# Down in two float32r passes for eight of eleven pieces, weights remade in tiles 2 to 7, x's row addition on GpSimd and one reciprocal for h and x

## The chip, the cores and the metric

The kernel runs on one core of one Trainium2 chip. The metric is the device time of the whole program in microseconds (us); the time before is 1699.41 us, the median of three runs (1698.96 to 1700.25). Engines are named as in the profile: PE is TensorE (PEld its weight loads), DVE is VectorE, ACT is ScalarE, POOL is GpSimd, and SP issues most DMAs. L1069 is line 1069 of the kernel file.

## What is computed

One block of a network: a gated linear scan, and then a feed-forward part whose rows and weights are rounded to FP4 in blocks of 16 values. Both are added to x through modulation vectors. Cut to what the change touches:

```
def fp4_quant_dequant(x):          # blocks of 16 along the last dim
    scale = max(abs(x) over the block) / 6, at least 1e-12
    xn = x / scale
    return GRID[searchsorted(MID, abs(xn))] * sign(xn) * scale

def fp4_linear(x, w):
    return einsum('bsk,nk->bsn', fp4_quant_dequant(x), fp4_quant_dequant(w))

x = x + ga * scan_part(layernorm(x) * (1 + ca) + sa)     # stage 1
h = layernorm(x) * (1 + cb) + sb                         # stage 2
h = silu(fp4_linear(h, w_gate)) * fp4_linear(h, w_up)    # 512 -> 1408
x = x + gb * fp4_linear(h, w_down)                       # 1408 -> 512
```

x has 2 x 4096 rows of 512 float32 values.

## The kernel before

Stage 1 (the scan) takes the first 528 us, and the first rows of x for stage 2 are rounded beside it. The change is in stage 2, the feed-forward part: a loop over 64 tiles of 128 rows. There the order of instructions on every engine, and on the DMA queues of SP and POOL, is the order in which the code issues them (`tc.manual_schedule`); no planner moves anything.

**Values in two parts.** FP4 values times their scales don't fit into one f16 number, so each of h, x and the weights is kept as a high and a low part, both f16. A product of one 128-wide piece of the contraction is then three f16 passes (high x high, high x low, low x high: `PASSES`). Where one side can be held in the type float32r, two passes do it (`TWO`): high x whole and low x remade, with the weights remade so that the cross terms come out right (a factor LAM or LAMX enters both sides).

**PE.** In iteration i PE runs `products(i)` (L1069): gate and up, three column groups of 480, 464 and 464 each, into six PSUM banks, over four pieces of 128. At first all four pieces take three f16 passes (72 matmuls). From tile 5 the last one, two and then three pieces take two float32r passes (`twos`, `wide`, `xw`), so a settled tile has 54. Then `down(i - 2)` (L1190) runs Down of the tile two before: 11 pieces of h, the first eight in three f16 passes and the last three in two f16 passes with LAM: 30 matmuls of 128x512. `hT` holds all of h transposed, both parts.

**The rest of a tile, in order.** ACT applies silu to each group (L1086); DVE makes the three gated products `hid` (L1091), which frees the PSUM banks for the next tile. On POOL, `out_times` (L1246) scales the Down result of an earlier tile, and `x_times` (L1115) multiplies the normalised x of the tile three ahead by its modulation; DVE adds the shift (`x_plus`, L1119). ACT casts the next tile's x to float32r (`xw`, L1050), and takes the mean and spread of the x four tiles ahead (L644, L650); POOL makes rstd and off (L652, L653, L1103).

Then h is rounded: DVE's block maxima (L136), scales `sb` (L117) and reciprocal (L132); ACT sums the scales (L123); POOL inverts the sum (`rt`, L125), makes `sl` in parts of 24 and of 64 columns (L1134, L1135), issues the output's accumulating DMA (`send`, L1232) and subtracts `sh` (L1141). DVE multiplies by the reciprocal (`xn`, L1146), ACT takes the absolute value (L1147), DVE rounds in two steps (L107, L109), ACT spreads the scales over 1024 columns (`se`, L1153, twice), and DVE forms the f16 parts (L1164, L1170, L1176) with one ACT copy between (L1166). SP issues the transpose of the parts (`hT`, L1185).

Between these lie the same steps for the x of the tile two ahead (reciprocal, L681, two roundings, L689, L697, its transpose `x2T` at L699), the block maxima of the x three ahead, and near the end of POOL's row that x's scales: `sb` (L117), then ACT's sum (L123) and `u` (L127), then `rt` and `sl` (L676). ACT reads the Down result from PSUM (`o`, L1241) and normalises the next x (`x_hat`, L1109).

**Remaking weights.** At i = 0, SP copies the gate and up weights to tiles of their own (`move_weights`, L1018), which frees the room for their float32r forms. In tiles 2 to 8 one gate or up piece at a time is remade: DVE adds its parts (L1034), ACT writes the rounded float32r form and a scaled one (L1038, L1039), DVE makes the second form (L1043).

Of the kernel before, what the change touches and what calls it, by code (L numbers as in the profile page):

```python
# [19 lines left out]
P = 128  # L20
D = 512
# [23 lines left out]
LAM = 81.0  # L45
LAMX = 101.0
TWOS = 3
MOVED = 2


@with_exitstack
def tile_adaln_block(
# [62 lines left out]
    def bounded(engine, am, nb):  # L115
        sb = small.tile([P, nb], F32, name="sb", tag=f"sb{nb}", bufs=2)
        engine.tensor_scalar(sb, am, 6e-12, TIE / 6.0, ALU.max, ALU.mult)  # L117
        return sb
# [11 lines left out]
    def inverse(sb, nb):  # L130
        inv = small.tile([P, nb], F32, name="inv", tag=f"inv{nb}", bufs=2)
        V.reciprocal(inv, sb)  # L132
        return inv
# [272 lines left out]
    DOWN = [(k, *p) for k in range(IC) for p in (PASSES if k * P < HSPLIT else TWO)]  # L406
# [122 lines left out]
    def quant_weight(wt, am, col, parts, hl):  # L529
# [17 lines left out]
        for at, by in parts:  # L547
            if by is None:
                A.copy(b1[:, at], xn[:, at])
            else:  # L550
                A.activation(b1[:, at], xn[:, at], AF.Copy, scale=by)
# [3 lines left out]
    def quant_rows(wt, i, am, col):  # L555
        dst = weights(("wgT", "wuT")[col], col, [P, 2 * KC, INTER])
        hl = new_hl()
        yield from quant_weight(wt, am, col, [(slice(0, D), None)], hl)
        S.dma_start_transpose(dst[:, :, i * P : (i + 1) * P], flat(hl))
# [6 lines left out]
    def quant_down(wt, i, j):  # L566
        n0, n1 = CHUNKS[j]
        w = n1 - n0
        dst = weights("wdT", 2, [P, 2 * IC, D])
        hl = flat(new_hl())[:, : 2 * w]  # L570
        two = hl.rearrange("p (a d) -> p a d", a=2)
        by = None if n0 < HSPLIT else (LAM - 1.0) / LAM
        yield from quant_weight(wt, am_d[i][j], 2, [(slice(0, w), by)], two)
        c = wd_chunk(0, n0 // P)
        S.dma_start_transpose(dst[:, c : c + 2 * w // P, i * P : (i + 1) * P], hl)
# [50 lines left out]
    NS = NBLK * KC  # L626
    qx, x1s, xst, gbs = {}, {}, {}, {}
# [31 lines left out]
    def twos(i):  # L659
        return min(max((i - MOVED - 1) // 2, 0), TWOS)  # L660

# [10 lines left out]
    def x_scales(h, am):  # L672
        sb = bounded(G, am, NBX)
# [3 lines left out]
        return h, sb, st, u  # L677

    def x_unit(h, sb, st, u):
        xn = work.tile([P, D], F32, name="xn", tag="xn512", bufs=1)  # L680
        V.tensor_tensor(blocks(xn), blocks(h), spread(inverse(sb, NBX), NBX), ALU.mult)  # L681
# [19 lines left out]

    ahead = {}

    def x_early(i, stage):
        if stage == 0:
            ahead[i] = x_scales(*x_norm(i))
        elif stage == 1:
            ahead[i] = x_unit(*ahead[i])
# [5 lines left out]
    EARLY = {NS - 3: [(0, 1)], NS - 2: [(0, 3), (1, 1)], NS - 1: [(1, 3)]}  # L714
    LATE = {NS - 4: [(0, 0)], NS - 3: [(0, 2), (1, 0)], NS - 2: [(1, 2)], NS: [(2, 0)]}
# [185 lines left out]
    with order:  # L901
# [3 lines left out]
        for slot in range(KC, NS + 3):  # L905
# [83 lines left out]
            if NS - 5 <= slot < NS - 1:  # L989
                n = slot - NS + 5  # L990
                xst[n] = stats_x(x1s[n])
            for n, stage in LATE.get(slot, []):
                x_early(n, stage)
            gate = cur
    tc.no_sync_barrier()
# [35 lines left out]
    def widen_sum(k, m):  # L1031
        hi, lo = moved[k][m]
        cv = ring.tile([P, INTER], F32, name="cv", tag="xnh")
        V.tensor_tensor(cv, hi, lo, ALU.add)  # L1034
        return k, m, cv

    def widen_high(k, m, cv):
        A.copy(wide[k][m][0], cv)  # L1038
        A.activation(cv, cv, AF.Copy, scale=LAMX)  # L1039

    def widen_low(k, m, cv):
        b1, b2 = wide[k][m]
        V.scalar_tensor_tensor(out=b2, in0=b1, scalar=1.0 - LAMX, in1=cv, op0=ALU.mult, op1=ALU.add)  # L1043

    def widen_rows(i):
        n = twos(i)
        if n:
            x2T = qx[i][0]
            xw = gring.tile([P, 2, n, P], F32R, name="xw", tag="xw", bufs=2)
# [30 lines left out]
    def brief():  # L1080
        return gring.tile([P, D], F32, name="silu", tag="silu", bufs=3)
# [18 lines left out]
    def x_off(i):  # L1100
        nm, rstd = xst[i]
        off = small.tile([P, 1], F32, name="off", tag="off")
        G.tensor_tensor(off, nm, rstd, ALU.mult)  # L1103
        xst[i] = rstd, off

    def x_hat(i):
        rstd, off = xst.pop(i)
        h = x1s.pop(i)
        A.activation(h, h, AF.Identity, bias=off, scale=rstd)  # L1109
        return i, h  # L1110

    def x_times(i, h):
        scale, by = mods_for(i * P // N)
        xm = brief()
        G.tensor_tensor(xm, h, scale, ALU.mult)  # L1115
        return h, xm, by

    def x_plus(h, xm, by):
        V.tensor_tensor(h, xm, by, ALU.add)  # L1119
# [4 lines left out]
    hb = HSPLIT // QB  # L1124

    def h_max(hid):
        am = small.tile([P, NBH], F32, name="amh", tag="amh", bufs=1)
        block_max(am, hid)
        return hid, bounded(V, am, NBH)

    def h_scales(sb):
        rt, u = total(sb, NBH, ud, 1)
        sl = small.tile([P, NBH], F32, name="sl", tag=f"sl{NBH}", bufs=2)
        G.tensor_scalar(sl[:, hb:], sb[:, hb:], rt, WPEAK * LAM, ALU.mult, ALU.mult)  # L1134
        G.tensor_scalar(sl[:, :hb], sb[:, :hb], rt, None, ALU.mult)  # L1135
        return rt, sl, u

    def h_parts(sb, rt, sl):
        sh = small.tile([P, hb], BF16, name="sh", tag="shh", bufs=2)
        A.activation(sh, sb[:, :hb], AF.Copy, scale=rt)  # L1140
        G.tensor_tensor(sl[:, :hb], sl[:, :hb], sh, ALU.subtract)  # L1141
        return sh

    def h_unit(hid, sb):
        xn = ring.tile([P, INTER], F32, name="xn", tag="xnh")
        V.tensor_tensor(blocks(xn), blocks(hid), spread(inverse(sb, NBH), NBH), ALU.mult)  # L1146
# [3 lines left out]
    def h_spread(sh, sl):  # L1150
        se = ring.tile([P, 2, HSPLIT], F16, name="se", tag="se")
        for n, src in enumerate((sh, sl[:, :hb])):
            A.activation(blocks(se[:, n, :]), spread(src, hb), AF.Copy, scale=WPEAK)  # L1153
            yield se
# [7 lines left out]
    def h_value(xn, nq, sl):  # L1162
        v = xn[:, HSPLIT:]
        V.tensor_tensor(blocks(v), blocks(nq[:, HSPLIT:]), spread(sl[:, hb:], NBH - hb), ALU.mult)  # L1164
        hl = ring.tile([P, 2, INTER], F16, name="hhl", tag="hhl")
        A.activation(hl[:, 0, HSPLIT:], v, AF.Copy, scale=1.0 / LAM)  # L1166
        return v, hl

    def h_low(i, nq, v, hl, se, u):
        V.tensor_tensor(  # L1170
            hl[:, :, :HSPLIT],
            nq[:, :HSPLIT].unsqueeze(1).to_broadcast([P, 2, HSPLIT]),
            se,
            ALU.mult,
        )
        V.scalar_tensor_tensor(  # L1176
            out=hl[:, 1, HSPLIT:],
            in0=hl[:, 0, HSPLIT:],
            scalar=1.0 - LAM,
            in1=v,  # L1180
            op0=ALU.mult,
            op1=ALU.add,
        )
        hT = ring.tile([P, 2 * IC, P], F16, name="hT", tag="hT", bufs=2)
        S.dma_start_transpose(hT, flat(hl))  # L1185
        qh[i] = hT, u

    def down_part(hT, pd, d):
        for n, (k, hp, wp) in enumerate(DOWN):
            T.matmul(  # L1190
                pd,
                hT[:, hp * IC + k, :],
                wdT[:, wd_chunk(wp, k), d],
                start=n == 0,
                stop=n == len(DOWN) - 1,
            )

    def down(i):
        hT, u = qh.pop(i)
        pd = side((P, D))  # L1200
        down_part(hT, pd, slice(0, D))
        return i, pd, u

    def last_down(i):

        hT, u = qh.pop(i)
        b, t0 = divmod(i * P, N)
        o = new_out()
        for n in range(2):
            d = slice(n * D // 2, (n + 1) * D // 2)  # L1210
            pd = bank(n)[:, : D // 2]
            down_part(hT, pd, d)
            scaled(o[:, d], pd, u, gbs[b][:, d])
# [3 lines left out]
    def new_out():  # L1217
        return ring.tile([P, D], F32, name="o", tag="o", bufs=2)

    def scaled(o, pd, u, by):  # L1220
        V.scalar_tensor_tensor(out=o, in0=pd, scalar=u, in1=by, op0=ALU.mult, op1=ALU.mult)  # L1221

    def gain_of(b):
        if b not in gbs:
            t = ring.tile([P, D], F32, name="mod_gb1", tag="mod_gb1")
            S.dma_start(t, modd[5][b : b + 1, :].to_broadcast([P, D]))
            gbs[b] = t
        return gbs[b]
# [4 lines left out]

    def finish(i, pd, u):
        o = new_out()
        scaled(o, pd, u, gain_of(i * P // N))
        send(i, o)
# [6 lines left out]
    def out_times(i, o):  # L1244
        ob = brief()
        G.tensor_tensor(ob, o, gain_of(i * P // N), ALU.mult)  # L1246
        return i, ob

    LAG, LEAD = 2, 2
# [5 lines left out]
    with tc.manual_schedule(engines={V.engine, A.engine, G.engine, S.engine, T.engine}):  # L1255
        ended, widening = [], None
        x = ahead.pop(LEAD)
        x1s[LEAD + 2] = load_x1(LEAD + 2)
        x_off(LEAD + 1)
        hat = x_hat(LEAD + 1)  # L1260
        scaled_out = []
        for i in range(NT):
            last = i == NT - 1
            work_i = products(i)
            downs = [] if i == NT - 2 else [i - LAG - 1, i - LAG] if last else [i - LAG]
# [5 lines left out]
            if i == NT // 4:  # L1271
                mods_for(1)
                gain_of(1)
# [5 lines left out]
            if widening is not None:  # L1279
                widen_high(*widening)  # L1280
            if not last:
# [4 lines left out]
            hid, sb = h_max(work_i[2])  # L1286
# [4 lines left out]
            if widening is not None:  # L1291
                widen_low(*widening)
                widening = None
            for o in outs:
                send(*o)
            xn = h_unit(hid, sb)
            if x is not None:
                x = x_unit(*x)
            sh = h_parts(sb, rt, hs)
            spreading = h_spread(sh, hs)  # L1300
            se = next(spreading)
            if nx is not None:
                nx = x_plus(*nx)
            if x is not None:
                x = x_round(i + LEAD, *x)
            next(spreading)
# [7 lines left out]
            scaled_out = [] if last else [out_of(*e) for e in ended]  # L1314
            hat = x_hat(i + LEAD + 2) if ahead_x else None
            v, hl = h_value(xn, nq, hs)
            h_low(i, nq, v, hl, se, u)
            x = nx
            if 0 <= i - MOVED < 2 * TWOS:
                k, m = KC - 1 - (i - MOVED) // 2, (i - MOVED) % 2  # L1320
                if m == 0:
                    widen_room(k)
                widening = widen_sum(k, m)
        last_x1 = load_x1(NT - 1)
        finish(*ended.pop(0))
        ended.append(down(NT - 2))
# [52 lines left out]
```

## Time and profile before

| | |
|---|---|
| time, median of three runs | 1699.41 us |
| the profiled execution's own time | 1701.52 us |
| its span in the profile | 1699.7 us |
| PE, DVE, ACT, POOL busy between 1000 and 1200 us | 200.0, 182.0, 131.8, 111.8 us |
| x_times on POOL (L1115, 128x512) | 1276 ns each, 61 of them |
| sl of 24 columns on POOL (L1134) | 1379 ns each, 64 of them |
| sl of 64 columns on POOL (L1135) | 449 ns each, 64 of them |
| cast of xw on ACT (L1050, 128x768) | 826 ns each, 55 of them |
| hT transpose, issue to landing | 5.2 us (median) |
| x2T transpose, issue to landing | 3.1 us (median) |

The span is one execution recorded by the hardware profiler, 1.8 us shorter than that execution's own time. A timeline line gives the start and the duration in us, the engine, the line, the operation, what it writes and reads, and, in brackets, how long the engine was idle before it and what ended this. A chain line gives start, duration, engine, result, line and the number of instructions. Durations of neighbouring instructions on DVE and ACT overlap by some 0.05 to 0.1 us, so the spacing of two starts is a little less than the duration.

### The profile page before, as it was taken

Reading aid. Unit: us, or ns where it says so; the run is one execution under the profiler, and the core shown is the slowest. Engines: PE = TensorE matmul, PEld = TensorE weight load, DVE = VectorE, ACT = ScalarE, POOL = GpSimd, SP = SyncE. Lnnn points to the kernel's source line nnn. Section 1 sums busy time; section 2 is a strip of 40 time slices with the busy share of each in tenths; the row PEclk is TensorE's granted clock in tenths of the full one; section 3 lists DMA queues with packets and bytes.
Section 4 is the critical chain, followed back from the end, with each engine's and each line's share of the span. In section 5 each row is a group of like instructions: output and inputs, shape, how many; then the busy total and the mean of one; then the engine's idle time right before and its main releaser. Section 6 shows DMA issues by size and latency. Waiting matters only on the chain.

```text
span 1699.7 us, 24145 instructions
## 1 busy us (share of the span) xinstructions
PE 1687.7 (99%) x8089; PEld 944.2 (56%) x8089; DVE 1490.2 (88%) x1927; ACT 1150.2 (68%) x2295; POOL 924.8 (54%) x1277
## 2 busy tenths in 40 slices
PE   9999999999999999999999999999999999999998
PEld 6444444444444445565666666666666566665664
DVE  7767889899985999998989989899898998998985
ACT  6676787788875667766666666666666666666652
POOL 5554555566654455655555555555555555555532
PEclk9999999999999999999999999999999999999999
DMA  7799979999976534445444444444444444444444
GB/s 249 177 243 218 201 184 204 186 206 199 207 153 183 114 70 82 80 81 95 97 93 86 78 95 78 88 86 83 95 78 83 89 83 94 79 80 94 73 82 72
DMA packets 471453, 208.92 MB, mean 123 GB/s; under 512 B 426470, under 2 KB 427750, under 8 KB 471328
## 3 DMA queue, kind: packets, MB, share of 16 engines
q1 hardware_dynamic: 456496, 173.85, 48.5%
q0 software_dynamic: 14544, 33.52, 11.1%
q8 instruction: 63, 1.03, 0.2%
q14 instruction: 62, 0.51, 0.1%
q10 hardware_dynamic: 288, 0.01, 0.0%
HBM read 62.86 MB, written 33.58 MB: 57 GB/s over the span
## 4 chain that ended last, share of the span: by engine, by line
PE 94%; DMA 2%; DVE 2%; ACT 1%; issue 1%; POOL 0%; DVEq 0%; POOLq 0%; SPq 0%; ACTq 0%
PE mm L1069 43%; PE mm L417 27%; PE sd L1190 23%; DMA gmax<-gsum 1%; DMA hT<-hhl 1%; DMA xT<-hl 0%; PE mm L1190 0%; PE mm L819 0%; DMA x2T<-hl 0%; ACT sq L370 0%; PE sd L220 0%; PE sd L234 0%; DVE ld L158 0%; ACT hl L383 0%; DVE xn L107 0%
## 5 line engine op out<-in xcount | busy, mean ns | idle before, releaser
L1069 PE MATMUL mm<-wide,xw 128*128 128x464 f32 (+1 forms) x2052 | 553.9, 403 | 0.0
L417 PE MATMUL mm<-xT,wqT 128*128 128x512 f16 (+1 forms) x2340 | 498.4, 376 | 0.8 <-DMA xT<-hl 0.8
L1069 PEld LDWEIGHTS mm<-wide,xw 128*128 128x128 f32 x2052 | 386.5, 188 | 72.5
L1190 PE MATMUL sd<-wdT,hT 128*128 128x512 f16 x1890 | 418.7, 379 | 1.7 <-DVE o L1221 1.7
L417 PEld LDWEIGHTS <-wqT 128*128 128x128 f16 x2340 | 228.6, 98 | 270.3 <-issue 1.7
L1069 PE MATMUL mm<-held,x2T 128*128 128x464 f16 (+1 forms) x1386 | 337.4, 365 | 3.0 <-DMA x2T<-hl 3.0
L1190 PEld LDWEIGHTS <-hT 128*128 128x128 f16 x1950 | 186.0, 98 | 226.8 <-issue 15.1
L1069 PEld LDWEIGHTS <-x2T 128*128 128x128 f16 x1530 | 126.3, 98 | 169.2 <-issue 71.1
L1091 DVE SCALAR_TENSOR_TENSOR hid<-mm,u,silu 128x464 f32<-128x464 f32 (+1 forms) x192 | 128.8, 701 | 79.4 <-PE mm L1069 69.3
L125 POOL TENSOR_TENSOR rt<-rms,mone 128x1 f32<-128x1 f32 x128 | 72.9, 569 | 221.7 <-ACT asb L123 221.7
L1147 ACT ACTIVATE hid<-xn 128x1408 f32<-128x1408 f32 x64 | 88.1, 1377 | 114.4 <-DVE xn L1146 114.4
L1086 ACT ACTIVATE silu<-mm,u 128x464 f32<-128x464 f32 (+1 forms) x192 | 116.3, 644 | 34.0 <-PE mm L1069 32.9
L453 ACT COPY yh<-y 128x1024 uint16<-128x1024 uint16 x64 | 66.9, 1045 | 68.8 <-DVE y L446 58.1
L652 POOL TENSOR_SCALAR rstd<-vs 128x1 f32<-128x1 f32 x118 | 25.2, 213 | 161.0 <-ACT sq L650 160.4
L107 DVE SCALAR_TENSOR_TENSOR xn<-hid,xn 128x1408 f32<-128x1408 f32 x64 | 103.6, 1619 | 2.9 <-ACT hid L1147 2.9
L1146 DVE TENSOR_TENSOR xn<-hid,inv 128x1408 f32<-128x1408 f32 x64 | 104.0, 1626 | 2.2
L136 DVE TENSOR_REDUCE amh<-hid 128x88 f32<-128x1408 f32 x64 | 103.7, 1620 | 2.2
L123 ACT ACTIVATE asb<-sb 128x88 f32<-128x88 f32 (+1 forms) x128 | 31.3, 245 | 107.9 <-DVE sb L117 105.1
L109 DVE SCALAR_TENSOR_TENSOR nq<-hid,xn 128x1408 f16<-128x1408 f32 x64 | 103.6, 1618 | 0.1
L1246 POOL TENSOR_TENSOR silu<-o,mod 128x512 f32<-128x512 f32 x32 | 41.2, 1288 | 100.3 <-DVE hid L1091 100.3
L435 DVE TENSOR_TENSOR_SCAN y<-sig,cy,mm 128x512 f32<-128x512 f32 x56 | 71.1, 1269 | 24.5 <-PE mm L417 21.2
L1134 POOL TENSOR_SCALAR sl<-sb,rt 128x24 f32<-128x24 f32 x64 | 88.3, 1379 | 6.3
(153 smaller groups left out, 2727.3 us busy)
## 6 DMA issues: line engine op xcount, KB each, us to landing
ld<-out_dram SPq DMA_DIRECT2D x65, 256.0 KB, 2.9
xr<-in_L_attn_x_dram SPq DMA_DIRECT2D x64, 256.0 KB, 3.7
out_dram<-xr POOLq DMA_DIRECT2D x64, 256.0 KB, 3.5
out_dram<-silu POOLq DMA_DIRECT2D x60, 256.0 KB, 4.0
scratch<-in_L_wmod_dram SPq DMA_DIRECT2D x24, 256.0 KB, 4.7
ld<-in_L_ffn_w_gate_dram SPq DMA_DIRECT2D x22, 256.0 KB, 3.1
ld<-in_L_ffn_w_up_dram SPq DMA_DIRECT2D x22, 256.0 KB, 3.3
ld<-in_L_ffn_w_down_dram SPq DMA_DIRECT2D x16, 256.0 KB, 3.5
```

The lines of the kernel that those rows point to most:

```text
L107: V.scalar_tensor_tensor(out=xn, in0=a, scalar=FLOOR, in1=xn, op0=ALU.max, op1=ALU.add)
L109: V.scalar_tensor_tensor(out=nq, in0=a, scalar=FLOOR, in1=xn, op0=ALU.max, op1=ALU.subtract)
L125: G.tensor_tensor(rt, rms, mone[:, :1], ALU.pow)
L136: V.tensor_reduce(am, src.rearrange("p (b k) -> p b k", k=QB), AX.X, ALU.max, apply_absolute_value=True)
L417: T.matmul(pp[:, t], wqT[e][:, wp, k, part, :], xT[:, xp * KC + k, t], start=n == 0, stop=n == 3 * KC - 1,)
L1069: T.matmul(pp[:, : n1 - n0], x2T[:, xp * KC + k, :] if k < k0 else xw[:, xp, k - k0, :], (rows_of(i, m, k) if k < k0 else wide[k][m])[wp][ ...
L1086: A.activation(sl[:, :w], pairs[j][0][:, :w], AF.Silu, scale=u[:, 0:1])
L1091: V.scalar_tensor_tensor(out=hid[:, n0:n1], in0=pairs[j][1][:, : n1 - n0], scalar=u[:, 1:2], in1=sl[:, : n1 - n0], op0=ALU.mult, op1=ALU.mult,
L1134: G.tensor_scalar(sl[:, hb:], sb[:, hb:], rt, WPEAK * LAM, ALU.mult, ALU.mult)
L1146: V.tensor_tensor(blocks(xn), blocks(hid), spread(inverse(sb, NBH), NBH), ALU.mult)
L1147: A.activation(hid, xn, AF.Abs, scale=MAGIC)
L1190: T.matmul(pd, hT[:, hp * IC + k, :], wdT[:, wd_chunk(wp, k), d], start=n == 0, stop=n == len(DOWN) - 1,)
```

## The change

- **Down.** From tile 7 (`DWIDE`) the first eight pieces (`KV`) take two float32r passes and the last three (`KR`) take three f16 passes: 25 matmuls instead of 30. Before tile 7 all eleven take three f16 passes (33). For the float32r passes ACT casts the transposed parts of h (`widen_h`, 128x2048) one iteration after h is made, between `x_hat` and the copies of the next h. Two transposes (`hrT`, `hvT`) take the place of one.
- **h's last steps.** The first 1024 columns are now multiplied by their scales in float32 in two halves, copied to f16 by ACT, and the low part is the difference; the last 384 are multiplied in f16 by the spread scales (which are now 384 wide).
- **Weights.** Eleven jobs, two in a tile, remake six gate and up halves and eight Down pieces in tiles 2 to 7. Five Down pieces go through DRAM (`far`), since their final place is free only at tile 8; POOL issues those transfers. Gate and up go to two passes one piece a tile, in tiles 4, 5 and 6.
- **x.** The shift of the normalised x is added on POOL, in place, directly after the multiplication. h and x share one tile of scales (`cell`) and one reciprocal of 120 columns. x's unit step now comes ahead of h's on DVE and ACT.
- **Buffers and order.** silu has two buffers instead of three, xw one instead of two; `o` uses another ring. Parts of the early x work of tile 2 move by a slot; its transpose is issued ahead of the weight copies. At the end the two last casts come ahead of the last h.

```diff
-LAM = 81.0
+KV = HSPLIT // P
+KR = IC - KV
+DWIDE = 7
...
     def twos(i):
-        return min(max((i - MOVED - 1) // 2, 0), TWOS)
+        return min(max(i - MOVED - 1, 0), TWOS)
...
+    def fetch_far():
+        t = ctile([P, 5, 2, D], F32R, "near", tag="weights2")
+        n = 0
+        for f in far:
+            w = f.shape[1]
+            G.dma_start(t[:, n : n + w], f)
+            n += w
...
+    def wide_jobs():
+        for k, m in ((3, 0), (3, 1), (2, 0), (2, 1)):
+            yield half(k, m)
+        yield pieces(6, 1, far[2])
+        for m in range(2):
+            yield half(1, m)
+        yield pieces(2, 2, far[0])
+        yield pieces(7, 1, None)
+        yield pieces(4, 2, far[1])
+        yield pieces(0, 2, None)
...
-            xw = gring.tile([P, 2, n, P], F32R, name="xw", tag="xw", bufs=2)
+            xw = gring.tile([P, 2, n, P], F32R, name="xw", tag="xw")
...
-        return gring.tile([P, D], F32, name="silu", tag="silu", bufs=3)
+        return gring.tile([P, D], F32, name="silu", tag="silu", bufs=2)
...
     def x_times(i, h):
         scale, by = mods_for(i * P // N)
-        xm = brief()
-        G.tensor_tensor(xm, h, scale, ALU.mult)
-        return h, xm, by
-
-    def x_plus(h, xm, by):
-        V.tensor_tensor(h, xm, by, ALU.add)
+        G.tensor_tensor(h, h, scale, ALU.mult)
+        G.tensor_tensor(h, h, by, ALU.add)
+        return h
...
-        G.tensor_scalar(sl[:, hb:], sb[:, hb:], rt, WPEAK * LAM, ALU.mult, ALU.mult)
-        G.tensor_scalar(sl[:, :hb], sb[:, :hb], rt, None, ALU.mult)
+        G.tensor_scalar(sl[:, :HB], sb[:, :HB], rt, WPEAK, ALU.mult, ALU.mult)
+        G.tensor_scalar(sl[:, HB:], sb[:, HB:], rt, None, ALU.mult)
...
+    def h_value(i, xn, nq, sl):
+        by = (LAMX - 1.0) / LAMX if i >= DWIDE else 1.0
+        hl = ring.tile([P, 2, HSPLIT], F16, name="hv", tag="hv")
+        for n, at in enumerate(HALVES):
+            b = slice(n * HB // 2, (n + 1) * HB // 2)
+            V.tensor_tensor(blocks(xn[:, at]), blocks(nq[:, at]), spread(sl[:, b], HB // 2), ALU.mult)
+            A.activation(hl[:, 0, at], xn[:, at], AF.Copy, scale=by)
+        return hl
...
+    def h_low(i, xn, hl, hrT, u):
+        for at in HALVES:
+            V.tensor_tensor(hl[:, 1, at], xn[:, at], hl[:, 0, at], ALU.subtract)
...
+    def widen_h(i, tag="hwT"):
+        make = ctile if tag != "hwT" else lambda *a, tag: ring.tile(*a[:2], name=a[2], tag=tag)
+        hwT = make([P, 2 * KV, P], F32R, "hwT", tag=tag)
+        A.copy(hwT, qh[i][0])
+        qh[i][0] = hwT
+
+    def down_part(i, pd, d):
+        hvT, hrT, _ = qh[i]
+        steps = []
+        for k in range(KV):
+            for hp, wp in PASSES if i < DWIDE else TWO:
+                w = wdT[:, wd_chunk(wp, k), :] if i < DWIDE else wide_d[k][wp]
+                steps.append((hvT[:, hp * KV + k, :], w))
+        for k in range(KR):
+            for hp, wp in PASSES:
+                w = wdT[:, wd_chunk(wp, KV + k), :] if i < DWIDE else rest[0][:, wp * KR + k, :]
+                steps.append((hrT[:, hp * KR + k, :], w))
...
             rt, hs, u = h_scales(sb)
-            if widening is not None:
-                widen_low(*widening)
-                widening = None
+            inv = inverse(cell, slice(0, None if x is not None else NBH))
             for o in outs:
                 send(*o)
-            xn = h_unit(hid, sb)
             if x is not None:
-                x = x_unit(*x)
+                x = x_unit(inv, *x)
+            xn = h_unit(hid, inv)
...
             hat = x_hat(i + LEAD + 2) if ahead_x else None
-            v, hl = h_value(xn, nq, hs)
-            h_low(i, nq, v, hl, se, u)
+            if DWIDE < i < NT - 2:
+                widen_h(i - 1)
+            hl = h_value(i, xn, nq, hs)
+            hrT = h_rest(nq, se)
+            h_low(i, xn, hl, hrT, u)
             x = nx
...
+            if i == DWIDE + LAG - 1:
+                fetch_far()
```

## The prediction

> **What bounds the kernel now.** I read the page first (busy shares, then the chain by line), then the chain in order of time, then the timeline of one tile on DVE, POOL and ACT.
>
> ```profile
> PE 1687.7 (99%) x8089; PEld 944.2 (56%) x8089; DVE 1490.2 (88%) x1927; ACT 1150.2 (68%) x2295; POOL 924.8 (54%) x1277
> PE mm L1069 43%; PE mm L417 27%; PE sd L1190 23%; DMA gmax<-gsum 1%; DMA hT<-hhl 1%; DMA xT<-hl 0%; PE mm L1190 0%; PE mm L819 0%; DMA x2T<-hl 0%; ACT sq L370 0%; PE sd L220 0%; PE sd L234 0%; DVE ld L158 0%; ACT hl L383 0%; DVE xn L107 0%
> 1014.97 6.49 PE sd L1190 x30
> 1021.46 11.29 PE mm L1069 x54
> ```
>
> PE sets the end: it is busy for 99%, and in the stage of the change the chain alternates between products (L1069) and Down (L1190). A settled tile (from tile 9) is 6.49 + 11.29 = 17.78 us. 88% for DVE is a mean; the tile's own slack is its one wait for PE:
>
> ```profile
> 1210.65 0.70 DVE L1091 SCALAR_TENSOR_TENSOR hid<-mm,u,silu 128x464 f32<-128x464 f32 x1 [1.25 <-PE mm L1069]
> 1228.43 0.70 DVE L1091 SCALAR_TENSOR_TENSOR hid<-mm,u,silu 128x464 f32<-128x464 f32 x1 [1.25 <-PE mm L1069]
> ```
>
> These third gated products stand 17.78 apart, and DVE waits 1.25 of it, so it works 16.53. The change takes work from PE; so POOL and ACT, which feed DVE, must be read too:
>
> ```profile
> 533.11 0.29 POOL L676 TENSOR_SCALAR sl<-sb,rt 128x32 f32<-128x32 f32 x1
> 1204.89 1.17 POOL L676 TENSOR_SCALAR sl<-sb,rt 128x32 f32<-128x32 f32 x1
> 1204.28 1.62 DVE L109 SCALAR_TENSOR_TENSOR nq<-hid,xn 128x1408 f16<-128x1408 f32 x1
> 644.62 1.01 POOL L1134 TENSOR_SCALAR sl<-sb,rt 128x24 f32<-128x24 f32 x1
> 644.88 0.68 DVE L1119 TENSOR_TENSOR ld<-silu,mod 128x512 f32<-128x512 f32 x1
> 218.87 1.29 POOL L472 TENSOR_TENSOR xr<-xr,y 128x512 f32<-128x512 f32 x1
> 219.36 1.35 DVE L388 SCALAR_TENSOR_TENSOR hl<-ld,rn,hl 128x512 f16<-128x512 f32 x1
> ```
>
> The same 128x32 operation takes 0.29 us with DVE idle and 1.17 beside L109, ending 0.16 after it. L1134, at 644.62, starts under one DVE operation with two inputs in SBUF (L681) and ends 0.07 after the next (L1119). The other way round, L388 (0.72 where POOL rests) is held to 0.55 past POOL's end. So the two engines exclude each other while DVE reads two SBUF operands; beside gated products (one input from PSUM), reduces and reciprocals POOL keeps its 1.28.
>
> ```profile
> 1201.03 0.65 POOL L117 TENSOR_SCALAR sb<-amx 128x32 f32<-128x32 f32 x1
> 1203.84 0.21 ACT L123 ACTIVATE asb<-sb 128x32 f32<-128x32 f32 x1
> 1206.60 0.52 ACT L1166 ACTIVATE hhl<-xn 128x384 f16<-128x384 f32 x1 [0.85 <-DVE xn L1164]
> ```
>
> POOL has x's scales (L117) 8.8 us after the third gated product starts (1192.9 to 1201.68). ACT comes to sum them at 1203.84 because of its own queue, and later still waits 0.85 for DVE. That is all the room POOL has.
>
> **The change, part by part.** *PE.* An f16 product costs 14.26/72 = 0.198 us (72 in an early tile); in 54, of which 36 are float32r, each float32r costs (11.29 - 54 x 0.198)/36 = 0.214, 16 ns more. Down has 6.49/30 = 0.216 per f16 matmul. Sixteen float32r and nine f16 give 16 x 0.232 + 9 x 0.216 = 5.66 (5.41 if float32r costs nothing more there). The tile becomes 16.95; tiles 7 to 63 save 57 x 0.83 = 47. Tiles 0 to 6 have 33 instead of 30: +7 x 0.65 = 4.5. The quicker ramp of gate and up gains six pieces, each (14.26 - 11.29)/3 = 0.99: -6. PE alone would end near 1651.
>
> *DVE.* From the spacing of one tile's rows: -0.72 (row addition), -0.38 (second reciprocal); h's last part falls from 0.48 + 1.13 + 0.47 to two values, one rest and two subtractions. By the rate of these rows (L1164 0.48 for 384; 0.60 for 512 float32; 1.13 for 2048 f16) that is 1.22 + 0.46 + 1.20. The reciprocal of 120 instead of 88 adds 0.20 (0.70 for 88, 0.35 for 32). Sum 16.43: DVE's work hardly shrinks, so 17.0 would be the tile with no new wait.
>
> *ACT.* The cast of h (128x2048) is new each tile. Between 768 elements (0.83, L1050) and 1408 (1.38, L1147) the slope gives 1.93. Two 512 copies (0.61 each) replace one of 384 (0.52); the spreads shrink from twice 1024 to twice 384. By busy time ACT has room. By order it doesn't: the cast stands between x's total and h's value copies, and DVE's subtractions need these copies.
>
> *POOL.* The addition adds 1.28 (row L1115), directly behind two others of this size. x_unit now stands ahead of xn and meets it.
>
> *One tile, from the start of the third gated product.* POOL's three tensor operations run to 3.9. DVE is at x_unit at 3.6 and held to 4.4 (row L388). POOL's rstd ends at 4.5; its power, caught behind xn (4.4 to 6.0), at 6.4; off 6.7; rt, behind x's first rounding, 7.6; the 64-wide scale 8.1. The 24-wide one behaves as at 644.62, held through x's product and h's first rounding: 10.25. The send's issue takes 0.7; the subtraction of sh is caught behind h's second rounding (10.7 to 12.3) and ends 12.45; x's scales end at 13.3. On ACT the waiting instruction is the sum of these scales. Queued behind it: that sum 0.33, u 0.20, o 0.57, x_hat 0.73, the cast 1.83, a value copy 0.6 (spacings). DVE's first subtraction starts 4.4 after x's scales, and behind it on DVE stand the second (0.6) and the gated products that free PE's banks: the next third one starts 7.0 after them. The tile is 13.3 + 7.0 = **20.3**. The bounds: every POOL operation slips in at the first gap, scales at 11.0, tile 18.0; one hold more, 14.3, tile 21.3. I take 20.3: 644.62 is the same operation in the same kind of gap.
>
> The Trainium skill, page "SBUF — State Buffer", section "SBUF: two separate sides", calls the port pair of DVE and GpSimd an exclusive lock, held for a whole instruction against DVE operations with two SBUF inputs; the rows above agree. Page "Perfetto Trace Analysis", section "Optimizing Scalar/DVE Operations", adds that offloading between these two might not help. By that sentence the moved addition is worth 0 instead of 0.72 per tile on DVE; by the rows it costs more, as POOL becomes late.
>
> *Tiles 2 to 7.* DVE's extra jobs, sum and low, take 3.1 for each of six halves of 1408 (spacing 1.54, row L1043 1.62) and by width 1.13 for each of eight pieces of 512: 27.6. 6 x 16.43 + 27.6 = 126.2, against 120.6 by PE before (3 x 20.7, 2 x 19.8, 18.8): +5.6; x_unit's hold 6 x 0.9 = 5.4; tiles 0 and 1 +1.3; the jobs' ACT passes ahead of h's copies, some 1: **+13** (bounds 8, without the hold, and 18, as much again for the POOL row after it). POOL's transfers of 2.6 MB: the 704 KB moves landed in 7.4 to 9.1 us, so some 30 us, longer than the tile that covers them: up to 5 of stall, only where the rest is fast.
>
> *Nothing:* tile 2's x transpose ahead of the weight moves on SP's queue: the moves (540.4 to 550.5 now) come behind tile 0's products, some 5 us later, and tile 1's last product starts only at 556.8 (without that cover, 5 once); one transpose more (hT 5.2 us, covered by the lag of two tiles; without it 3); one xw buffer: the cast moves from 1.1 before the end of products to behind it, and Down's 5.66 covers it (without it, 0.8 per tile); two silu buffers: POOL's output product still starts beside the third gated one.
>
> *End.* Two casts of h on the last path, 1.9 each; last Down, before 60 matmuls in 6.74, has 32 float32r whose weight loads take 0.188 each (row PEld L1069) and 18 at 0.112: 8.0, +1.3. Together +5.1; two tiles without x's work go at PE's pace, -1.7.
>
> **Sum.** Span 1699.7 + 13 + 52 (tiles 8 to 59) x (20.3 - 17.78) - 1.7 + 5.1 = 1847. The profiled execution took 1701.5, 1.8 over its span and 2.1 over the median of 1699.4; with both shifted alike (+147.4), the forecast on the median's scale is 1847.
>
> **Rivals.** *A, faster: POOL's lateness is hidden.* For it: ACT came 2.2 us after POOL's scales (1201.68 to 1203.84), and the spreads shrink by some 0.5 each. Against: the addition (1.28) and the cast (1.93) spend that. If POOL ends by 10.0, the tile is 17.0: 1699.4 + 9 - 52 x 0.78 + 2 (end) + 2 (fetch) = 1672. *B, milder: POOL slips in at first gaps,* tile 18.0: 1699.4 + 16.4 + 52 x 0.22 = 1727. For it: L117 before was held 0.65 and not longer. *C, one hold more,* 21.3: 1899. *D: float32r passes on h save nothing.* With weight loads of 0.188 (row PEld) bare, 16 x 0.42 + 9 x 0.216 = 8.7, tile 20.0 by PE alone: 1699.4 + 57 x 2.2 - 1.5 = 1823. Against: in products the loads lie under 0.214 each. The point from which slower decides: tile 17.78 - 16.4/52 = 17.5, x's scales at 10.5.
>
> **How the numbers follow.** Forecast 0.42, C 0.10, B 0.20, D 0.03, A 0.22, and 0.03 for a tile that lands on 17.5. About 0.2% is what a measurement here can tell from no change. Faster 0.22, same 0.03, slower 0.75. The range 1670 to 1905 leaves out half of A and the top of C; the forecast's own range is 1790 to 1905 (tiles 19.3 to 21.4).
>
> **What would show it.** PE idle in every tile from 8 on, released by DVE's gated products; DVE's idle before the first subtraction, ended by ACT's value copy; ACT's idle before the sum of x's scales, ended by POOL; the 24-wide scale's mean above 1.4; Down near 5.7 a tile; x_unit above 0.8. It is wrong if PE stays above 97% (A), if Down takes 8 (D), or if POOL's x scales end by 10.5.

## The result

The changed kernel takes 1851.66 us (median of four runs, 1851.21 to 1852.72) against 1699.83 for the kernel before (median of four): ratio 1.0891, 95% interval 1.0872 to 1.0909, 152 us slower. The forecast was 1847. Its profiled execution has a span of 1850.9 us.

The page of the changed kernel, first the busy shares, then the chain by engine and by line:

```profile
PE 1701.2 (92%) x7784; PEld 1030.3 (56%) x7784; DVE 1519.3 (82%) x1940; ACT 1246.8 (67%) x2431; POOL 1163.9 (63%) x1347
POOL 36%; PE 28%; DVE 14%; ACT 13%; issue 7%; DMA 3%; SPq 0%; ACTq 0%; POOLq 0%; DVEq 0%
PE mm L420 25%; POOL sl L1185 5%; POOL rstd L652 5%; ACT hwT L1243 5%; DVE hid L1155 4%; POOL silu L1301 4%; POOL sl L1191 4%; POOL ld L1167 4%; POOL ld L1166 3%; DVE hv L1234 3%; POOL out_dram L1292 3%; POOL cell L122 2%; POOL off L706 2%; ACT ld L712 2%; POOL rt L129 2%
```

No engine but PE is near full, and PE has left the chain: its 28% is nearly all stage 1 (L420). In stage 2 the chain goes through POOL, ACT and DVE. Here is one tile of it, in order of time (start, duration, engine, result, line):

```profile
999.11 1.27 POOL ld L1167
1000.46 0.52 POOL rstd L651
1001.05 1.81 POOL rstd L652
1002.94 0.76 POOL off L706
1003.70 0.51 POOL rt L129
1004.30 0.30 POOL sl L1184
1004.71 2.12 POOL sl L1185
1006.83 0.90 POOL out_dram L1292
1007.74 1.22 POOL sl L1191
1009.05 0.81 POOL cell L122
1009.89 0.33 ACT asb L127 x2
1010.24 0.29 ACT u L131
1010.54 0.42 ACT o L1296
1011.01 0.80 ACT ld L712
1011.82 1.79 ACT hwT L1243
1013.61 0.54 ACT hv L1220
1014.17 0.56 DVE hv L1234
...
1016.01 0.70 DVE hid L1155
1016.79 1.29 POOL silu L1301
```

It is a closed loop. POOL's twelve operations end with x's scales (`cell`, L122) at 1009.86; ACT sums them and has four more things in its queue, the cast of h (`hwT`, 1.79) among them, before h's copies; DVE subtracts, makes the gated products, and the second of them lets POOL begin again. Third gated products start at 996.6 and 1016.9: 20.30 us a tile, before 17.78. The 24-wide `sl` (L1185), a few columns, takes 2.12: it starts beside one of DVE's operations with two inputs in SBUF and ends 0.14 after the next. The rows of the timeline, and the waits of ACT and of DVE in this tile:

```profile
1004.42 0.74 DVE L690 TENSOR_TENSOR xn<-hl,sl 128x512 f32<-128x512 f16 x1
1005.08 1.61 DVE L110 SCALAR_TENSOR_TENSOR xn<-hid,xn 128x1408 f32<-128x1408 f32 x1
1008.99 0.52 ACT L1203 ACTIVATE se<-sl 128x384 f16<-128x384 f32 x1 [2.66 <-POOL sl L1191]
1014.17 1.29 DVE L1234 TENSOR_TENSOR hv<-xn,hv 128x512 f16<-128x512 f32 x2 [3.42 <-ACT hv L1220]
```

| kernel | time, us | tile, us (settled) | third gated product of tile 8 starts, us |
|---|---|---|---|
| before | 1699.83 | 17.78 | 696.5 |
| changed | 1851.66 | 20.30 | 714.4 |
| e1: row addition back on DVE | 1732.35 | 17.74 | 713.8 |
| e2: cast of h behind the copies | 1851.82 | 20.17 | 712.8 |
| e4: x's scales on DVE | 1838.26 | 19.82 | 713.7 |
| e5: before, with the addition on POOL | 1702.95 | 17.78 | 698.9 |
| e6: one more product on POOL | 1921.88 | 21.39 | 718.5 |
| e7: POOL's output product in place | 1857.08 | 19.94 | 724.7 |
| e8: cast ahead of the spreads | 1768.53 | 18.51 | 712.8 |
| e9: three silu buffers | 1721.81 | 17.62 | 712.7 |
| e10: e9, e8 and another end | 1723.11 | 17.64 | 713.7 |
| e11: e10, and POOL's and ACT's order | 1689.84 | 16.99 | 713.8 |

Times of e1 to e10 are single runs, beside runs of the kernel before at 1699.3 to 1702.4; e11 has four.

### The profile page after: what moved, and what is told of

Read it like the earlier page. It is cut to its first block, busy times and chain, and to the rows that moved or that the text cites. A ratio compares the mean times of both kernels' runs of the same rounds, so it can differ in the third digit from the quotient of the medians.

```text
span 1850.9 us, 24034 instructions
## 1 busy us (share of the span) xinstructions
PE 1701.2 (92%) x7784; PEld 1030.3 (56%) x7784; DVE 1519.3 (82%) x1940; ACT 1246.8 (67%) x2431; POOL 1163.9 (63%) x1347
## 4 chain that ended last, share of the span: by engine, by line
POOL 36%; PE 28%; DVE 14%; ACT 13%; issue 7%; DMA 3%; SPq 0%; ACTq 0%; POOLq 0%; DVEq 0%
PE mm L420 25%; POOL sl L1185 5%; POOL rstd L652 5%; ACT hwT L1243 5%; DVE hid L1155 4%; POOL silu L1301 4%; POOL sl L1191 4%; POOL ld L1167 4%; POOL ld L1166 3%; DVE hv L1234 3%; POOL out_dram L1292 3%; POOL cell L122 2%; POOL off L706 2%; ACT ld L712 2%; POOL rt L129 2%
## 5 line engine op out<-in xcount | busy, mean ns | idle before, releaser
L420 PE MATMUL mm<-xT,wqT 128*128 128x512 f16 (+1 forms) x2340 | 498.2, 376 | 1.6 <-DMA xT<-hl 1.6
L1133 PEld LDWEIGHTS mm<-wide,xw 128*128 128x128 f32 x2124 | 402.0, 190 | 92.8 <-ACT xw L1114 18.3
L420 PEld LDWEIGHTS <-wqT 128*128 128x128 f16 x2340 | 228.7, 98 | 270.8 <-issue 2.5
L1301 POOL TENSOR_TENSOR silu<-o,mod 128x512 f32<-128x512 f32 x63 | 81.7, 1297 | 310.4 <-DVE hid L1155 297.0
L1234 DVE TENSOR_TENSOR hv<-xn,hv 128x512 f16<-128x512 f32 x128 | 84.9, 705 | 171.8 <-ACT hv L1220 171.8
L1258 PE MATMUL sd<-part,hwT 128*128 128x512 f32 x336 | 115.0, 456 | 118.6 <-ACT hwT L1243 108.7
L1258 PE MATMUL sd<-near,hwT 128*128 128x512 f32 x560 | 166.2, 451 | 3.3 <-DMA near<-far 3.3
L1258 PEld LDWEIGHTS sd<-part,hwT 128*128 128x128 f32 x336 | 66.5, 211 | 151.0 <-ACT hwT L1243 128.4
L652 POOL TENSOR_TENSOR rstd<-rstd,mhalf 128x1 f32<-128x1 f32 x118 | 141.6, 1200 | 9.8
L1258 PEld LDWEIGHTS sd<-near,hwT 128*128 128x128 f32 x560 | 126.6, 226 | 36.8 <-DMA near<-far 4.7
L1203 ACT ACTIVATE se<-sl 128x384 f16<-128x384 f32 x64 | 33.3, 521 | 137.7 <-POOL sl L1191 137.7
L1258 PE MATMUL sd<-rest,hrT 128*128 128x512 f16 x504 | 119.7, 383 | 0.0
L1185 POOL TENSOR_SCALAR sl<-cell,rt 128x24 f32<-128x24 f32 x64 | 113.8, 1779 | 5.8
```

The source lines that it names most:

```text
L420: T.matmul(pp[:, t], wqT[e][:, wp, k, part, :], xT[:, xp * KC + k, t], start=n == 0, stop=n == 3 * KC - 1,)
L652: G.tensor_tensor(rstd, rstd, mhalf[:, 0:1], ALU.pow)
L1133: T.matmul(pp[:, : n1 - n0], x2T[:, xp * KC + k, :] if k < k0 else xw[:, xp, k - k0, :], (rows_of(i, m, k) if k < k0 else wide[k][m])[wp][ ...
L1185: G.tensor_scalar(sl[:, HB:], sb[:, HB:], rt, None, ALU.mult)
L1234: V.tensor_tensor(hl[:, 1, at], xn[:, at], hl[:, 0, at], ALU.subtract)
L1258: T.matmul(pd, h, w[:, d], start=n == 0, stop=n == len(steps) - 1)
```

## The experiments

**e1, the addition back on DVE.**

```diff
     def x_times(i, h):
-        G.tensor_tensor(h, h, by, ALU.add)
-        return h
+        return h, by
-    def x_max(h):
+    def x_max(h, by):
+        V.tensor_tensor(h, h, by, ALU.add)
```

> The changed kernel with x's row addition back on DVE, ahead of the block maxima. My theory (POOL, 20.3 us a tile, is late because of three tensor operations and of DVE holding its small ones): POOL's tensor operations end 1.3 earlier, off and rt get by before x_unit as they did in the changed kernel's tile 10, x's scales are ready near 9 us after the third gated product instead of 13.2, and the tile is DVE's work, 16.43 + 0.68 = 17.1: 1675 to 1700 us. Rival 'the cast's place on ACT decides by itself': 1.3 less at most, 19.0 a tile, near 1785. Rival 'float32r on PE or its lower clock decides': unchanged, 1852.

1732.35 us and 17.74 a tile: the mechanism holds, the size is off by 0.6 a tile. POOL has x's scales 8.7 us after the third gated product, about as expected (9). But DVE's own list is 17.36 (17.75 less 0.22 of idle for ACT's copy and 0.17 for the third silu), not 17.1. So without POOL's lateness a tile still gains only 0.04 over the kernel before, and tiles 0 to 7 lose 17. The time is over that of the kernel before.

**e2 and e8, the cast of h elsewhere on ACT.** Each differs from the changed kernel only in where `widen_h(i - 1)` stands. The first of the two places added below is e8's, the second e2's:

```diff
+            if DWIDE < i < NT - 2:
+                widen_h(i - 1)
             se = h_spread(sh, hs)
...
-            if DWIDE < i < NT - 2:
-                widen_h(i - 1)
             hl = h_value(i, xn, nq, hs)
+            if DWIDE < i < NT - 2:
+                widen_h(i - 1)
```

> The changed kernel with the cast of h (widen_h) behind the two value copies on ACT instead of ahead of them. My theory: the cast's 1.9 us leaves the way from x's scales to the gated products, POOL stays as it is, and the tile is 13.2 + 5.1 = 18.4: near 1755 us (1745 to 1775). Rival 'POOL alone sets the tile': 1852. Rival 'the cast is the only cause': 17.1 a tile, 1690.

1851.82: a miss. DVE's two waits in e2's timeline, before the subtractions and before the gated products:

```profile
1010.21 1.29 DVE L1234 TENSOR_TENSOR hv<-xn,hv 128x512 f16<-128x512 f32 x2 [1.62 <-ACT hv L1220]
1013.08 1.33 DVE L1155 SCALAR_TENSOR_TENSOR hid<-mm,u,silu 128x480 f32<-128x480 f32 x2 [1.57 <-ACT silu L1150]
```

DVE's wait before the subtraction fell from 3.42 to 1.62, and 1.57 came up before the gated products: the cast (1.89) now stands ahead of the silus. I had left out the rest of ACT's queue. e8 puts the cast where ACT waits for POOL anyway.

> The changed kernel with the cast of h ahead of the spreads on ACT, where ACT stands 2.66 us idle for POOL's subtraction of sh. Moved behind the copies the cast only moved the wait from DVE's subtraction to the silus (20.17 a tile). My theory: both times it lies between x's scales and the next gated products; in the idle stretch it does not, and the tile is 20.3 - 1.9 = 18.4: near 1752 us (1740 to 1770). Rival 'POOL alone sets the tile, the cast costs nothing': 1852.

1768.53, 18.51 a tile (18.4 expected; the time is at the top of the expected range). x's scales still come 13.3 after the third gated product, and from there to the next it is 5.2 instead of 7.0. So the loop has two causes that add: POOL's row (13.3), and behind it ACT's queue with DVE's last steps (7.0, the cast 1.8 of it).

**e4, x's scales on DVE** (`bounded(V, sb, am)` in the place of `bounded(G, sb, am)`).

> The changed kernel with x's scales (one small operation) on DVE instead of POOL. In the trace ACT waits 2.66 us for POOL's subtraction of sh ahead of the second spread, and only 0.37 more for x's scales. If the whole row of POOL's operations is late, ACT gains only these 0.4 and the tile is 19.9: 1830 us (1815 to 1852). If x's scales themselves are the wait, as the prediction's words have it, the tile falls below 18: under 1740.

1838.26, 19.82 a tile: 0.48 gained. The scales are only the last of POOL's row; with them gone, ACT waits for the subtraction of sh just ahead of them.

**e6, one more multiplication on POOL** (x times its modulation twice).

```diff
         G.tensor_tensor(h, h, scale, ALU.mult)
+        G.tensor_tensor(h, h, scale, ALU.mult)
         G.tensor_tensor(h, h, by, ALU.add)
```

> The changed kernel with one more 128x512 multiplication on POOL (x is multiplied by its modulation twice, which changes the values). My theory: POOL's row shifts by 1.3, x_unit on DVE is held that much longer, and the tile is 21.6: 1915 to 1930 us. Rivals in which POOL is not on the path: 1852.

1921.88: an operation of 1.28 on POOL costs 1.09 a tile, nearly all of it. The hold on DVE isn't on x_unit, as I had expected (0.72 there), but on the operation behind it, h's `xn` (2.71 instead of 1.61).

**e5, the kernel before with the addition alone.**

```diff
         G.tensor_tensor(xm, h, scale, ALU.mult)
+        G.tensor_tensor(h, xm, by, ALU.add)
...
-        V.tensor_tensor(h, xm, by, ALU.add)
```

> The kernel before with one part of the change alone: x's row addition on POOL, behind the multiplication. There PE sets the tile, POOL's output product starts 1.8 us ahead of the third gated product, so the third tensor operation would end near +2.05, ahead of xn (+2.9). My theory says that the addition hurts by its place in POOL's row, not as such: same time as before, 1699 to 1705 us, DVE's idle per tile 1.25 + 0.7 = about 2.0. Rival 'two engines that exclude each other gain nothing and lose the difference': +0.6 a tile over DVE's slack, 1705 to 1740.

1702.95, the same 17.78 a tile. The moved addition is harmless by itself: there POOL's output product starts 2.0 ahead of the third gated product (0.1 in the changed kernel), and POOL's last tensor operation ends at 2.2 instead of 3.8. Its DVE row waits 1.5 for PE instead of 1.25, less than the 2.0 expected, since it also waits 0.38 for ACT.

**e9, three silu buffers.** The room comes from h's rest, written over the spread scales.

```diff
-        return gring.tile([P, D], F32, name="silu", tag="silu", bufs=2)
+        return gring.tile([P, D], F32, name="silu", tag="silu", bufs=3)
...
-        hr = ring.tile([P, 2, INTER - HSPLIT], F16, name="hr", tag="hr")
-            hr, nq[:, HSPLIT:].unsqueeze(1).to_broadcast([P, 2, INTER - HSPLIT]), se, ALU.mult
-        S.dma_start_transpose(hrT, flat(hr))
+            se, nq[:, HSPLIT:].unsqueeze(1).to_broadcast([P, 2, INTER - HSPLIT]), se, ALU.mult
+        S.dma_start_transpose(hrT, flat(se))
```

> The changed kernel with three silu buffers again (the room comes from h's rest, now multiplied in place): POOL's output product waits for the first gated product, not the second, and the third silu for none. My theory: POOL's row starts 0.66 earlier and ends its tensor operations at 3.2, ahead of x_unit at 3.6, so the small operations fall into the gaps that they caught in tile 27 of the changed kernel: 18.3 a tile or less, 1720 to 1755 us. If only the 0.66 counts: 19.6, 1817. If not POOL: 1852.

1721.81, 17.62 a tile, better than expected. POOL starts 0.6 earlier behind the first gated product. Counted from the third, its tensor operations end at 3.4 (3.2 expected) instead of 3.8, and x's scales at 9.6 instead of 13.3. The tile is 2.7 shorter. The changed kernel shows the same by itself: its tile 27 took 18.27 between neighbours of 20.3. There POOL isn't earlier; DVE is later, for it stands idle 0.46 ahead of its reciprocal (as in tile 27 of e7, e9 and e11; why is open). The timeline of the tile before it and of tile 27:

```profile
1080.46 0.90 DVE L136 RECIPROCAL inv<-cell 128x120 f32<-128x120 f32 x1
1081.65 0.51 POOL L651 TENSOR_SCALAR rstd<-vs 128x1 f32<-128x1 f32 x1
1090.24 0.80 POOL L122 TENSOR_SCALAR cell<-amx 128x32 f32<-128x32 f32 x1
```

```profile
1101.11 0.90 DVE L136 RECIPROCAL inv<-cell 128x120 f32<-128x120 f32 x1 [0.46 <-DVE cell L122]
1101.94 0.19 POOL L651 TENSOR_SCALAR rstd<-vs 128x1 f32<-128x1 f32 x1
1108.67 0.65 POOL L122 TENSOR_SCALAR cell<-amx 128x32 f32<-128x32 f32 x1
```

The tiles start at 1077.8 and 1098.1, so the reciprocal starts at 2.7 and at 3.05, and POOL's tensor operations end at 3.8 in both. rstd gets by ahead of x_unit in the second (0.19 instead of 0.51), the small operations after it find earlier gaps (the 24-wide `sl` takes 0.67 instead of 2.12), and the scales end at 11.3 instead of 13.3. The next third gated product follows at 18.3, 7.0 behind the scales as ever.

**e7, POOL's output product in place** (`G.tensor_tensor(o, o, gbs[...])`, no buffer to wait for).

> The changed kernel with POOL's output product written in place, so that it waits for no silu buffer and no gated product; it can start as soon as the Down result is there. My theory: the row of POOL ends 1.3 or more earlier, x_unit is held no more, the small operations get by in their first gaps: tile 17.0 to 18.4, 1685 to 1755 us, with some DVE time lost where the product now lies beside h's last steps (two operands in SBUF). If the buffer's wait does not matter: 1852.

1857.08, a miss that shows the other side. POOL's small operations do find their early gaps (scales 8.7 after the third gated product), but its large ones now lie beside h's last steps:

```profile
1017.20 2.37 DVE L1219 TENSOR_TENSOR xn<-nq,sl 128x512 f32<-128x512 f16 x2
1017.34 1.68 POOL L1300 TENSOR_TENSOR o<-o,mod 128x512 f32<-128x512 f32 x1
1019.49 1.63 DVE L1225 TENSOR_TENSOR hr<-nq,se 128x768 f16<-128x768 f16 x1
```

DVE's two values take 2.37 instead of 1.31, the rest 1.63 instead of 0.55, the subtractions 2.38 instead of 1.29: some 3.2 a tile. The product's wait for gated products was cover, not only a wait.

**e10 and e11, a better order.** e10 joins e8 and e9 and moves the cast for tile 62 behind the absolute value of the last h. e11 adds:

```diff
-            outs = [out_times(*o) for o in scaled_out]
             nx = x_times(*hat) if hat is not None else None
+            outs = [out_times(*o) for o in scaled_out]
...
-            hat = x_hat(i + LEAD + 2) if ahead_x else None
             hl = h_value(i, xn, nq, hs)
+            hat = x_hat(i + LEAD + 2) if ahead_x else None
```

> Three silu buffers, the cast of h ahead of the spreads, and at the end the cast for tile 62 behind the absolute value of tile 63's h instead of ahead of its scales. With three silu buffers alone a tile took 17.61 and DVE was idle 0.2 of it; DVE's scale operation (L122) was held 0.9 under POOL's addition. My theory: the cast's place gives back the 0.2, DVE's own list stays, 17.4 a tile, and the end is 5 us shorter: near 1705 us (1698 to 1712). Rival 'without the cast on ACT's way PE sets the tile': 17.0, 1685.

1723.11, a miss: 17.64 a tile. With POOL early, ACT no longer stands idle ahead of the spreads, so the cast still lies on its way and DVE waits 0.19 for the copies as before. The end gains 2.5, not 5, and the step from tile 9 to tile 10 takes 23.97, 2.3 more than in e9.

> As the last, and x_hat behind the value copies on ACT, and on POOL x's two operations ahead of the output product. Then POOL's tensor operations start beside h's last subtraction and end about where DVE comes to its scale operation, which is no longer held. My theory: DVE's list falls to some 16.7, PE sets the tile at 16.95 to 17.1: 1678 to 1695 us, faster than the kernel before (1699). Rival 'the hold only moves to the subtractions': 17.4 and more, 1705 or over.

1689.84 (1688.25 to 1690.75) against 1701.03 for the kernel before, measured beside it (seven runs): ratio 0.9935, interval 0.9918 to 0.9951. It is faster than both kernels, than the kernel before by 0.65%. What e9 left is one DVE operation under POOL's addition; the lines of e9, then those of e11:

```profile
1000.32 1.27 POOL L1167 TENSOR_TENSOR ld<-ld,mod 128x512 f32<-128x512 f32 x1
1000.53 1.12 DVE L122 TENSOR_SCALAR cell<-amh 128x88 f32<-128x88 f32 x1
```

```profile
1010.44 1.31 POOL L1300 TENSOR_TENSOR silu<-o,mod 128x512 f32<-128x512 f32 x1
1012.06 0.21 DVE L122 TENSOR_SCALAR cell<-amh 128x88 f32<-128x88 f32 x1
```

In e11 POOL's third tensor operation ends at 1011.75, ahead of DVE's scales, which take 0.21 again. The tile is 16.99, PE's own 16.95. PE is busy for 98% of e11's span, and its chain by engine has PE back:

```profile
PE 85%; DVE 7%; issue 2%; DMA 2%; ACT 2%; POOL 1%; SPq 0%; ACTq 0%; DVEq 0%; POOLq 0%
```

## Why the prediction was right, point by point

- **The loop.** Third gated product to x's scales 13.3 (predicted 13.3), scales to the next 7.0 (7.0), tile 20.30 (20.3). e6 and e8 move the two parts separately, by 1.1 and by 1.8.
- **x_unit's hold** was wrong. x_unit starts at 3.6 and ends at 4.4, as predicted, but it does so nearly unheld: 0.73 in the tile above (1000.19), against 0.69 in e1, where POOL's last operation of 128x512 ends 1.2 us ahead of it. The sign "above 0.8" didn't come. The collision is on POOL's side: rstd takes 0.51 (0.19 in e1) and its power 1.81 (0.55 in e1).
- **Which wait ends last.** I named x's scales. e4 shows that the whole row of POOL is meant: moving them gains 0.48. And PE's idle time is not ended by DVE's gated products, as I had named it: from 800 to 1760 us every wait of PE above 0.3 us is ended by ACT's cast of h.
- **PE.** In the settled tile float32r Down took 5.74 (5.66) where PE ran at full clock. e11's 16.99 agrees with 16.95, the sum of Down and products, and rules out rival D. The formula for a float32r product should have read (11.29 - 18 x 0.198)/36 = 0.215; the 16 ns are right.
- **The cast** took 1.89 (1.93), the 24-wide scale 1.78 on average.
- **Sum, in spans** (before 1699.7, changed 1850.9: 151.2 against 147.4 predicted). Three terms are off, by -4.7, +4.9 and +3.6, and partly cancel: that the total is so close is in part luck.
  - Tiles 8 to 59: 126.3 (131), mainly since tiles 10, 27 and 57 took 17.00, 18.27 and 17.96.
  - Tiles 2 to 7: 13.0 (12), but not for the reasons given. The 5.4 for x_unit's hold isn't there: x_unit takes 0.69 to 0.70 in each of these tiles. In its place DVE waits 5.9 for ACT, 4.2 of it in tile 7.
  - Tiles 0 and 1: 4.9 (1.3). In tile 1 DVE is busy for 19.8 of 20.35: the first weight job adds 1.6, and two of h's last steps, beside POOL's multiplication and addition, take 1.76 and 1.62 instead of 0.69 and 0.55. The moved weights, which I had taken as hidden, do stop PE for 1.8 there, but PE has the next products done 7 us ahead of the third gated product, so this costs nothing.
  - The end: 7.0 (3.4). The cast of tile 62 waited 7.1 for PE on ACT's queue, ahead of the last h, and DVE's rounding of that h waited 7.6 behind it. I had priced the casts and not their wait.
- **Rival A** gave 1672 for a kernel without POOL's lateness. e1 and e9 reach 17.74 and 17.62 a tile, not 17.0: that rival's tile left out what DVE waits for and is held by. It takes e11's order to reach 16.99. The 17 lost in the first tiles stay, and so does a stall near tile 9, where PE waits for the Down pieces from DRAM (0.9 and 2.6 us in e11). My outer range, 1670 to 1905, took in half of this rival, so the time alone tells little; the rows of the tile tell the two apart.
- **The sentence of the Trainium skill** (page "Perfetto Trace Analysis", section "Optimizing Scalar/DVE Operations") that offloading between DVE and GpSimd might not help: in the changed kernel the addition on POOL costs 119 us (1851.7 against e1's 1732.4). With three silu buffers it no longer does: e9's tile is 17.62, e1's 17.74. In e11 it lies beside gated products and block maxima, and the tile is 16.99; with DVE's list of e1 (17.36) it would be some 0.4 longer, an estimate, for no run has e11 with the addition on DVE. The place decides.

## What to carry to other kernels

Before an operation goes from DVE to POOL, write down POOL's whole row of a tile, mark which DVE operations it lies beside, and follow the queue behind the engine that waits for its last result. An operation moved along one queue only moves the wait, unless it lands in a stretch where that engine stands idle for another reason. A wait may be cover: taking away a buffer's wait let large POOL operations start earlier, against DVE operations that they block.

## What the runs showed that was not expected

A shift of 0.3 to 0.4 us between POOL's row and DVE's changes the tile by 2 to 2.7 us (tile 27, where DVE is late, and e9, where POOL is early), since POOL's small operations then find earlier gaps. And DVE's TENSOR_SCALAR with one input (128x88) is held by POOL too, 1.12 us against 0.21. The Trainium skill, page "SBUF — State Buffer", section "SBUF: two separate sides", counts DVE operations in a 2-port mode to the lock beside those with two inputs, which would fit this row; reduces and reciprocals beside POOL's operations kept their 1.62 and 0.90.

PE's Down differs by tile in the changed kernel. Here are the windows that hold it in two tiles, after PE waited 1.62 and 3.09 us for the cast (start and end, length, busy times of PE, PEld, DVE, ACT and POOL, granted clock, DMA share, GB/s):

```profile
1013.60:1019.40 5.80, 5.74 (x25) 3.83 (x26) 4.99 (x7) 4.95 (x11) 2.53 (x3) 1.00 0.59 61
1033.90:1041.20 7.30, 7.25 (x25) 5.03 (x26) 6.36 (x9) 5.61 (x14) 3.95 (x4) 0.77 0.50 108
```

After 1.62 us of idleness Down took 5.74 at a granted clock of 1.00; after 3.09 it took 7.25 at 0.77. It isn't so after every wait of this length: of 26 waits of 3.0 to 3.1 us between 800 and 1760 us, 20 were followed by a clock of 0.65 to 0.79 and six by 1.00 (at 851.27, for one). What tells them apart is open. The lost 1.5 lies where PE waits anyway: the tiles take 20.3 either way.
